# An eighth of layer 2's softmax tokens turned and summed by TensorE, and layer 3 added to the output by GpSimd's DMA

## The chip, the core and the metric

The program runs on one core of a Trainium2 chip. A core has five engines with instruction queues of their own: PE (TensorE, matrix products), DVE (VectorE), ACT (ScalarE), POOL (GpSimd) and SP (SyncE, which here only issues transfers). Each takes its instructions in order. Transfers between DRAM and the on-chip memory SBUF run on 16 DMA engines; PE writes its products to PSUM, where DVE and ACT read them. The metric is the device time of one execution in microseconds (us), as the median of several runs.

## The reference

x holds 16 images of 64x64 tokens with 256 channels, fp32. Four layers follow each other, each of the form x = x + layer(groupnorm(x)):

```
x = x + L0(gn(x))   # nearest of 1024 code vectors, by token
x = x + L1(gn(x))   # attention along each row of the image, sigmoid in place of softmax
x = x + L2(gn(x))
x = x + L3(gn(x))   # linear attention, 4 heads of 32, projected and layer-normed

def L2(x):                                # n = 4096 tokens of an image
    x0, x1, x2 = x @ w1 + b1, x @ w2 + b2, x @ w3 + b3    # one number per token each
    sim = x0[:, :, None] * x1[:, None, :]                 # n x n
    sm = softmax(sim, axis=1)                             # over the first n
    feats = einsum('bn,bnm->bm', x2, sm)
    return sigmoid(feats)[..., None] * x

def L3(x):
    q, k, v = split(x @ w_qkv)
    q = softmax(q, over the head's 32) * 32 ** -0.5
    k = softmax(k, over the tokens)
    o = (k.T @ v, by head) applied to q, then @ w_out + b_out
    return layernorm(o) * gamma + beta
```

So layer 2 takes 4096 x 4096 exponentials per image, their sum over the first index (the denominator) and their sum weighted by x2 (the numerator).

## The kernel before

An image (in the code a batch, `b`) is 8 chunks of 512 tokens. Except in the first layer's output, activations lie with channels on the 128 partitions, as two halves of 128 channels by 512 tokens (`[P, NK, CW]`, 512 KB a chunk). Each stage reads its input from a DRAM buffer and writes its output to one.

- `stats0` (L313) reads x and takes the statistics of the first group norm.
- `stage1` (L329) is the search: 32 steps per batch. A step has four fp32 matmuls into a 1024-column PSUM tile `pd` (L403), a sum and maximum on DVE (L409), the index of the maximum (L414), and a gather by POOL that adds the code vectors to the tokens (L415). `back` (L374) turns a finished chunk.
- `layer1` (L441) does the row attention. Its `ph` and `po` tiles are the other users of 1024-column PSUM tiles, of which there are two (`ps_w`, L68); the four 512-column ones come from `ps_m` (`bank`).
- `rows2` (L567) makes x0, x1 and x2 for the batch and writes them to DRAM; `spread_rows` (L610) reads x0 and x2 back, repeated on all partitions, 2048 tokens at a time (two halves).
- `stage2` (L620) is the softmax. A tile has 128 values of the second index on the partitions and 2048 of the first along the row. ACT takes the exponentials with x1 as the factor and the row's sum as a by-product (L645); DVE multiplies by x2 and sums (L648). There are 32 x 2 such tiles per batch, in three buffers `ex`. Then the gate is made and stored.
- `gate2` (L681) applies the gate, takes statistics, and stores the residual x3 to DRAM (L709).
- `stage3` (L717) is layer 3. A first pass over the chunks loads x3 (L760) and makes keys, queries, values and the context; `put_row` puts the constant row `x_row` together (L788). A second pass, the out pass, makes the output: for each pair of 128 tokens PE turns x3 back to tokens on the partitions (L902), adds the projection (L908) and the constant row (L912); ACT copies the sum out of PSUM to `y` (L913) and SP stores it (L923, L926). The scale by token comes from `form`, `variance` and `deviate` (L855 to L870), with a power on POOL (L868).

The stages of up to several batches run beside each other. Every stage is a generator that yields costs; at the end of the kernel a heap interleaves them by planned start and length (L925 to L968), and the framework's scheduler then orders each engine's instructions. SP's queue holds nearly all loads and stores, and a transfer that has to wait holds up those behind it. POOL's queue holds the gathers, layer 3's differences and products on the queries (L802, L756) and the powers.

The lines that the out pass and the softmax turn on:

```
nc.scalar.activation(
    ex, x0b, AF.Exp, bias=nmax[:, T : T + 1], scale=x01[:, T, 1:2], accum_out=den[:, h, T : T + 1]
)
...
nc.tensor.matmul(px, lhsT=ones3, rhs=twice(x_row), start=False, stop=True, skip_group_check=True)
nc.scalar.copy(y[:, 2 * pr : 2 * pr + 2, :], px)
```

## Time and profile before

| | |
|---|---|
| median of 3 runs (5653.28 to 5692.56) | 5671.16 us |
| the profiled execution | 5674.06 us |
| its span, first to last instruction | 5672.1 us |
| mean granted TensorE clock | 0.962 |
| moved by DMA, HBM read and written | 751.18 MB and 303.04 MB |
| waits of POOL's gathers for their indices (L415 for L414) | 1337.5 us |

Times are in us unless marked ns. PEld is PE's loading of weights, which overlaps its products. In a line of a group stand the source line, the engine, the operation, the output and inputs by name, the shapes, and the count; behind the bar the busy time of all, the mean ns of one, the idle time of the engine just before them, and what ended that idle time. A wait line names who waited for whom, the total, how often and the longest. SPq and POOLq are the queues that issue transfers. Matmuls overlap: the mean ns of one is longer than the time from one start to the next.

### The profile page before, as it was taken

To read this page: it belongs to the slowest core of one execution; us is meant where nothing else is said; L and a number is where in the kernel's file an instruction comes from. 1 tells how busy PE (TensorE), PEld (TensorE's weight loads), DVE (VectorE), ACT (ScalarE), POOL (GpSimd) and SP (SyncE) were. 2 spreads that over 40 slices of the span, in tenths; PEclk is the share of its full clock that TensorE was granted. 3 is DMA by queue.
4 is the path that set the end of the run, shared out by engine and by line. 5 is a ranking of instruction groups with operands and counts; after the bars stand their busy time and mean duration, and the time that the engine had idled before them with its cause. 6 is when DMAs were issued, how large, how long until landed. Compare 5 with 4: busy or idle time off the path is not lost.

```text
span 5672.1 us, 76096 instructions
## 1 busy us (share of the span) xinstructions
PE 5162.0 (91%) x26927; PEld 3189.6 (56%) x26927; DVE 5049.3 (89%) x7186; ACT 4571.1 (81%) x6642; POOL 1801.5 (32%) x1076
## 2 busy tenths in 40 slices
PE   7977889989999999999999999999999999987788
PEld 3534446545656566565655656565565656564556
DVE  7589799899999999999999999999999999988882
ACT  4468589888989898888978888898888879887873
POOL 2223234323333333334333333333333333321221
PEclk9988999999999999999999999999999999998889
DMA  8553744655665757566575656657575675745543
GB/s 254 174 178 84 232 115 144 214 163 185 196 198 175 224 159 236 171 211 198 185 234 155 216 185 200 210 173 236 160 224 183 201 219 156 222 149 176 200 157 119
DMA packets 521365, 1059.26 MB, mean 187 GB/s; under 512 B 52504, under 2 KB 266392, under 8 KB 512792
## 3 DMA queue, kind: packets, MB, share of 16 engines
q1 hardware_dynamic: 406288, 885.11, 46.5%
q0 software_dynamic: 73728, 67.14, 8.3%
q10 hardware_dynamic: 40968, 102.13, 4.6%
q8 instruction: 214, 3.51, 0.3%
q14 instruction: 167, 1.37, 0.1%
HBM read 751.18 MB, written 303.04 MB: 186 GB/s over the span
## 4 chain that ended last, share of the span: by engine, by line
PE 46%; DVE 17%; ACT 16%; issue 6%; DMA 5%; POOL 4%; SPq 0%; ACTq 0%; DVEq 0%; POOLq 0%
PE pd_s L403 14%; ACT ex_s L645 7%; DVE ex_s L648 7%; PE ph_l L493 4%; PE pxo_s L908 3%; PE pqv_s L782 3%; PE po_l L533 2%; PE pk_s L765 2%; ACT nn_s L398 2%; POOL qv_s L802 2%; PE pz_s L857 2%; DVE i_s L414 2%; DVE nn_s L409 2%; PE pxo_s L902 2%; PE pvr_s L865 2%
## 5 line engine op out<-in xcount | busy, mean ns | idle before, releaser
L648 DVE CUSTOM_DVE_ANT_0 ex_s<-ex_s,x2b 128x2048 f32<-128x2048 f32 x1024 | 2360.4, 2312 | 77.6 <-ACT ex_s L645 74.6
L645 ACT ACTIVATE ex_s<-x0b,nmax_s,x_r 128x2048 f32<-128x2048 f32 x1024 | 2138.6, 2089 | 40.7 <-DVE num_s L648 30.5
L403 PE MATMUL pd_s<-e,xn_s 128*128 128x512 f32 x4096 | 1971.1, 614 | 43.9 <-DVE m L409 27.9
L415 POOL DMA_INDIRECT xc_s<-in_emb_rows,i_s x512 | 1113.7, 2175 | 1852.7 <-DVE i_s L414 1337.5
L403 PEld LDWEIGHTS pd_s<-e,xn_s 128*128 128x128 f32 x4096 | 745.8, 195 | 778.8 <-issue 669.1
L409 DVE CUSTOM_DVE_ANT_0 nn_s<-pd_s,nn_s 128x1024 f32<-128x1024 f32 x512 | 619.9, 1212 | 113.5 <-PE pd_s L403 63.0
L414 DVE FIND_INDEX8 i_s<-m,nn_s 128x8 uint32<-128x1024 f32 x512 | 622.9, 1217 | 0.0
L398 ACT ACTIVATE nn_s<-ne,nx_s 128x1024 f32<-128x1024 f32 x512 | 582.5, 1143 | 33.1 <-DVE nx_s L369 18.7
L493 PE MATMUL ph_l<-wh_l,xt_l 128*128 128x256 f32 x2048 | 519.6, 390 | 28.7 <-DVE m L409 16.9
L782 PE MATMUL pqv_s<-wqv_s,xk_s 128*128 128x256 f32 x2048 | 489.3, 381 | 0.0
L493 PEld LDWEIGHTS ph_l<-wh_l,xt_l 128*128 128x128 f32 x2048 | 379.7, 192 | 138.9 <-issue 69.0
L782 PEld LDWEIGHTS pqv_s<-wqv_s,xk_s 128*128 128x128 f32 x2048 | 389.1, 191 | 120.6 <-issue 59.7
L802 POOL TENSOR_TENSOR qv_s<-qv_s,qm_s 128x512 f32<-128x512 f32 x128 | 221.6, 1731 | 662.6 <-DVE qm_s L801 363.2
L868 POOL TENSOR_TENSOR lrs_s<-lrs_s,mhalf 128x4 f32<-128x4 f32 x128 | 178.0, 1391 | 677.2 <-ACT lrs_s L867 663.3
L756 POOL TENSOR_TENSOR qv_s<-qv_s,qd_s 128x512 f32<-128x512 f32 x128 | 214.4, 1675 | 249.0 <-DVE qd_s L755 132.0
L533 PE MATMUL po_l<-blk,h_l 128*128 128x128 f32 x2048 | 282.1, 288 | 3.0 <-DVE m L409 1.5
L533 PEld LDWEIGHTS po_l<-blk,h_l 128*128 128x128 f32 x2048 | 260.6, 200 | 41.1 <-issue 24.5
L908 PE MATMUL pxo_s<-wctx_s,qo_s 128*128 128x256 f32 x1024 | 269.2, 386 | 2.2 <-DVE qo_s L876 2.2
L765 PE MATMUL pk_s<-xk_s,wk_s 128*128 128x512 f32 x512 | 256.0, 620 | 1.0 <-DMA xk_s<-x_g 0.9
L913 ACT COPY y_s<-pxo_s 128x512 f32<-128x512 f32 x256 | 147.5, 580 | 132.4 <-PE pxo_s L912 116.0
L378 PE MATMUL pt_s<-ident,xc_s 128*128 128x128 f32 x1024 | 156.7, 282 | 105.2 <-DMA xc_s<-in_emb_rows,i_s 79.0
L351 ACT ACTIVATE sq_s<-xt_s,first 128x512 f32<-128x512 f32 x256 | 200.2, 806 | 37.2 <-DMA x0b<-rows_r 21.0
(206 smaller groups left out, 7322.0 us busy)
## 6 DMA issues: line engine op xcount, KB each, us to landing
xs_s<-in_xT SPq DMA_DIRECT2D x128, 512.0 KB
xt_s<-in_xT SPq DMA_DIRECT2D x128, 512.0 KB
xc_s<-in_x SPq DMA_DIRECT2D x128, 512.0 KB
x_s<-xt_s ACTq DMA_DIRECT2D x128, 512.0 KB
xt_l<-x_s SPq DMA_DIRECT2D x128, 512.0 KB
x_l<-xt_l SPq DMA_DIRECT2D x128, 512.0 KB
xr_r<-x_l SPq DMA_DIRECT2D x128, 512.0 KB
xg_g<-x_l SPq DMA_DIRECT2D x128, 512.0 KB
```

The costliest lines, as they stand in the source:

```text
L398: nc.scalar.activation(nn, ne2, AF.Identity, bias=nx2[ch][:, t : t + 1])
L403: nc.tensor.matmul(pd[:, cols], lhsT=xn[ch][:, k, t * P : (t + 1) * P], rhs=e2[:, k, cols], start=(k == 0), stop=(k == NK - 1),)
L409: nc.vector.tensor_tensor_reduce(out=nn, in0=pd, in1=nn, scale=1.0, scalar=-3.0e38, op0=ALU.add, op1=ALU.max, accum_out=m8[:, 0:1],)
L414: nc.vector.max_index(i8, m8, nn)
L415: nc.gpsimd.indirect_dma_start(out=xc[ch][:, t, :], out_offset=None, in_=emb_rows, in_offset=bass.IndirectOffsetOnAxis(ap=i8[:, 0:1], axis=0),
L493: nc.tensor.matmul(ph[:, t, :], lhsT=X[:, k, t * P : (t + 1) * P], rhs=wh_n[:, k, :], start=(t % 2 == 0 and k == 0), stop=False, skip_grou ...
L533: nc.tensor.matmul(po[:, m : m + P], lhsT=h[:, t, k * P : (k + 1) * P], rhs=at[:, t, :, :].rearrange("p r i -> p (r i)"), start=True, stop ...
L645: nc.scalar.activation(ex, x0b, AF.Exp, bias=nmax[:, T : T + 1], scale=x01[:, T, 1:2], accum_out=den[:, h, T : T + 1])
L648: nc.vector.tensor_tensor_reduce(out=ex, in0=ex, in1=x2b, scale=1.0, scalar=0.0, op0=ALU.mult, op1=ALU.add, accum_out=num[:, h, T : T + 1],)
L765: nc.tensor.matmul(pk, lhsT=wk_n[:, k, :], rhs=xt[:, k, :], start=(k == 0), stop=(k == NK - 1))
L782: nc.tensor.matmul(pqv[:, j, :], lhsT=xt[:, k, t * P : (t + 1) * P], rhs=wqv_n[:, k, :], start=(j == 0 and k == 0), stop=False, skip_group ...
L908: nc.tensor.matmul(px[:, j, :], lhsT=qT[:, t * P : (t + 1) * P], rhs=wctx[:, 1, :], start=False, stop=False, skip_group_check=True,)
```

## The change

Layer 2: the last 4 of the 32 groups of 128 tokens of the first index (an eighth, `SHARE`) leave the tiles of the second half, which become 1536 wide. For them the matrix is formed turned: first index on the partitions, second along the row. `parts_of_rows` splits x1, the negated maximum and x0 into three bf16 parts each, sends the parts through DRAM to 12 partitions, and `outer` makes their products and sums in PSUM, 1024 columns at a time. ACT takes the plain exponential (`powers`), PE sums over the partitions with a column of x2 and one of ones (`contract`), ACT copies, PE turns the rows back and DVE sums four parts (`collect`). Each of the 8 chunks of the second index gets one such sequence, spread over the steps of the softmax.

Layer 3: `gate2` stores its residual straight to the output, which now lies in chunks with channels on the partitions. The out pass no longer loads x3, turns it or adds the constant row. It makes the projection with channels on the partitions, ACT adds the constant as a bias by partition, and a transfer that POOL issues adds the chunk to what lies in the output. The output is put in the reference's order after the launch, where it is reshaped.

```
+SHARE = 4
+SHARES = {}
+PROD = 12
...
+    spread = const.tile([P, 2, P], BF16, name="spread")
+    nc.gpsimd.memset(spread, 0.0)
+    for g in range(4):
+        nc.gpsimd.memset(spread[32 * g : 32 * g + PARTS], 1.0)
+    pair = const.tile([P, 8, 32], F32, name="pair")
+    nc.gpsimd.memset(pair, 0.0)
+    nc.gpsimd.memset(pair[:, :, 1], 1.0)
...
     def spread_rows(rd, b, h):
+        width = TOK // 2 - (P * SHARES.get(b, SHARE) if h == 1 else 0)
...
     def stage2(b, parts=1):
...
+        sums = small.tile([P, 2, 3, NT], F32, tag="sums", name=f"sums_{tag}", bufs=1)
...
+        def parts_of_rows():
+            nc.vector.tensor_copy(cat[:, 0:NT], x01[:, :, 1])
+            nc.vector.tensor_copy(cat[:, 2 * NT : 2 * NT + K], x01[:, NT - K :, 0])
+            nc.vector.tensor_copy(pair[:, 0:K, 0], x01[:, NT - K :, 2])
+            n = 2 * NT + K
+            pp = bank(f"pcat_{tag}")
+            nc.tensor.transpose(pp[:n, :P], cat[:, :n], ident)
+            bits = small.tile([2 * NT + 8, PARTS, P], BF16, tag="bits", name=f"bits_{tag}", bufs=1)
+            for m in range(PARTS):
+                nc.vector.tensor_copy(bits[:n, m, :], pp[:n, :P])
+                if m + 1 < PARTS:
+                    nc.vector.tensor_tensor(pp[:n, :P], pp[:n, :P], bits[:n, m, :], ALU.subtract)
+            ud = dram.tile([1 + PARTS, PARTS, NT, P], BF16, tag="ud", name=f"ud_{tag}")
+            nc.sync.dma_start(out=ud[0].rearrange("m t p -> t m p"), in_=bits[NT : 2 * NT])
+            for m in range(PARTS):
+                nc.sync.dma_start(out=ud[1 + m].rearrange("m t p -> t m p"), in_=bits[0:NT])
+            vd = dram.tile([PARTS, PARTS, 8, P], BF16, tag="vd", name=f"vd_{tag}")
+            for m in range(PARTS):
+                nc.sync.dma_start(out=vd[:, m, 0:K].rearrange("m t p -> t m p"), in_=bits[2 * NT : n])
+            for g in range(4):
+                nc.sync.dma_start(
+                    out=spread[32 * g + PARTS : 32 * g + PROD, 0 : K // 4, :],
+                    in_=vd.rearrange("i m (e g) p -> (i m) g e p", g=4)[:, g, 0 : K // 4, :],
+                )
+            return ud
+
+        def begin(c):
+            u = s2p.tile([P, CW], BF16, tag="uu", name=f"uu_{tag}_{c}", bufs=2)
+            src = ud.rearrange("i m t p -> (i m) (t p)")[:, c * CW : (c + 1) * CW]
+            for g in range(4):
+                nc.sync.dma_start(out=u[32 * g : 32 * g + PROD, :], in_=src)
+            others[c] = u
+
+        def outer(c, n):
+            e, q = divmod(n, 2)
...
+            pw = wide(f"pet_{tag}_{c}_{n}")
+            for r in range(2):
+                g = 2 * q + r
+                rows = slice(32 * g, 32 * g + PROD)
+                nc.tensor.matmul(
+                    pw[:, r * CW : (r + 1) * CW], lhsT=spread[rows, e, :], rhs=u[rows, :], start=True, stop=True
+                )
+            banks[c, n] = pw
+
+        def powers(c, n):
+            e, q = divmod(n, 2)
+            if q == 0:
+                others[c].append(s2p.tile([P, TOK // 2], F32, tag="ex", name=f"et_{tag}_{c}_{e}", bufs=3))
+            nc.scalar.activation(others[c][-1][:, 2 * q * CW : 2 * (q + 1) * CW], banks.pop((c, n)), AF.Exp)
+
+        def contract(c):
+            pn = bank(f"pn_{tag}_{c}")
+            for e in range(K // 4):
+                for g in range(4):
+                    nc.tensor.matmul(
+                        pn[32 * g : 32 * g + 32, :], lhsT=pair[:, 4 * e + g, :],
+                        rhs=others[c][1 + e][:, g * CW : (g + 1) * CW], start=(e == 0), stop=(e == K // 4 - 1),
+                    )
+            nc.scalar.copy(others[c][-1][:, 0:CW], pn)
+
+        def collect(c):
+            row = others.pop(c)[-1]
+            pt = bank(f"pnt_{tag}_{c}")
+            for t in range(CH):
+                nc.tensor.transpose(pt[:, t * P : (t + 1) * P], row[:, t * P : (t + 1) * P], ident)
+            nc.vector.tensor_reduce(
+                sums[:, :, 2, c * CH : (c + 1) * CH].rearrange("p r t -> p t r"),
+                pt.rearrange("p (t j n) -> p t n j", j=4, n=32)[:, :, 0:2, :], AX.X, ALU.add,
+            )
...
-                    yield 2.4
+                    yield 2.4 * width / (TOK // 2)
+                    c = part + step // 8
+                    n = step % 8
+                    if K == 0:
+                        pass
+                    elif n <= K // 2:
+                        if n > 0:
+                            powers(c, n - 1)
+                            yield 1.2
+                        if n < K // 2:
+                            outer(c, n)
+                    elif n == 5:
+                        contract(c)
+                        if c + 1 < NCHUNK:
+                            begin(c + 1)
+                    elif n == 7:
+                        collect(c)
+                    step += 1
...
     def gate2(b):
...
-            d = dram.tile([P, NK, CW], F32, tag=f"x3_{ch}", name=f"x3_{tag}_{ch}", bufs=3)
-            nc.sync.dma_start(out=d, in_=xt)
-            x3.append(d)
+            nc.sync.dma_start(out=dst[ch], in_=xt)
...
     def stage3(b):
...
-            if ch == 0:
-                put_row(x_row, xm_, by_identity, f"x_{tag}", idle=8)
...
-            xt = xb.tile([P, NK, CW], F32, tag="xb", name=f"xo_{tag}_{ch}")
-            nc.sync.dma_start(out=xt, in_=x3[ch])
             qT = qs[ch]
-            y = s3p.tile([P, CH, C], F32, tag="u4", name=f"y_{tag}_{ch}")
-            for pr in range(2):
+            y = s3p.tile([P, NK, CW], F32, tag="u4", name=f"y_{tag}_{ch}")
+            for pr in range(NK):
                 if pr == 1 and ch + 1 < NCHUNK:
                     deviate(ch + 1)
-                px = bank(f"pxo_{tag}_{ch}_{pr}").rearrange("p (j c) -> p j c", c=C)
-                for j in range(2):
-                    t = 2 * pr + j
-                    for k in range(NK):
-                        nc.tensor.matmul(
-                            px[:, j, k * P : (k + 1) * P], lhsT=xt[:, k, t * P : (t + 1) * P], rhs=ident,
-                            is_transpose=True, start=(j == 0 and k == 0), stop=False, skip_group_check=True,
-                        )
-                for j in range(2):
-                    t = 2 * pr + j
-                    nc.tensor.matmul(
-                        px[:, j, :], lhsT=qT[:, t * P : (t + 1) * P], rhs=wctx[:, 1, :], start=False, stop=False,
-                        skip_group_check=True,
-                    )
-                nc.tensor.matmul(px, lhsT=ones3, rhs=twice(x_row), start=False, stop=True, skip_group_check=True)
-                nc.scalar.copy(y[:, 2 * pr : 2 * pr + 2, :], px)
+                px = bank(f"pxo_{tag}_{ch}_{pr}")
+                nc.tensor.matmul(px, lhsT=wctx[:, 1, pr * P : (pr + 1) * P], rhs=qT, start=True, stop=True)
+                nc.scalar.activation(y[:, pr, :], px, AF.Identity, bias=xm_[:, pr : pr + 1])
...
-                    if before is not None:
-                        nc.sync.dma_start(out=dst[:, (ch - 1) * CH : ch * CH, :], in_=before)
+                    nc.gpsimd.dma_start(out=x3[ch], in_=y, accum_op=ALU.add)
```

## The prediction

> **What bounds the kernel now.** I read the page's busy times first, then the busy times by stretch, the waits of PE and DVE in the steady stretch, the groups by line in that stretch, and last the timeline of PE in the middle and at the end.
>
> ```profile
> PE 5162.0 (91%) x26927; PEld 3189.6 (56%) x26927; DVE 5049.3 (89%) x7186; ACT 4571.1 (81%) x6642; POOL 1801.5 (32%) x1076
> ```
>
> Over the whole span PE and DVE are close together. The stretch from 1500 to 4900 us says more (columns: length, then busy us of PE, weight loads, DVE, ACT, POOL, then PE clock, DMA share, GB/s):
>
> ```profile
> 1500.00:4900.00 3400.00, 3222.50 (x17247) 2013.05 (x17246) 3187.87 (x4508) 2910.59 (x4229) 1169.16 (x669) 0.99 0.63 197
> ```
>
> The groups in the same stretch:
>
> ```profile
> L648 DVE CUSTOM_DVE_ANT_0 ex_s<-ex_s,x2b 128x2048 f32<-128x2048 f32 x656 | 1513.5, 2311 | 55.9 <-ACT ex_s L645 53.3 <-issue 2.5
> ...
> L908 PE MATMUL pxo_s<-wctx_s,qo_s 128*128 128x256 f32 x692 | 178.0, 380 | 0.0
> L765 PE MATMUL pk_s<-xk_s,wk_s 128*128 128x512 f32 x320 | 153.0, 596 | 1.0 <-DMA xk_s<-x_g 0.9
> L902 PE MATMUL pxo_s<-ident,xo_s 128*128 128x128 f32 x688 | 106.9, 275 | 0.0
> ...
> L912 PE MATMUL pxo_s<-x_row,ones 128*128 128x512 bf16 x173 | 65.6, 379 | 0.0
> ...
> L593 PE MATMUL pr_r<-xr_r,wrow_n 128*32 128x512 f32 x320 | 46.2, 601 | 0.0
> ...
> L645 ACT ACTIVATE ex_s<-x0b,nmax_s,x_r 128x2048 f32<-128x2048 f32 x656 | 1370.1, 2089 | 11.1 <-DVE nmax_s L632 6.5 <-DVE num_s L648 3.2
> ```
>
> A batch has 64 of the L648 products, so 656 of them are 10.25 batches, 331.7 us each. Per batch PE is busy 314.4 us (94.8%), DVE 311.0 (93.8%), ACT 284.0 (85.6%), POOL 114.1. Neither of the first two alone is the bound: each idles some 6%. What ends their waits:
>
> ```profile
> DVE ex_s L648 <- ACT ex_s L645: 53.3, 42, 2.8
> DVE nn_s L409 <- ACT nn_s L398: 25.2, 40, 2.2
> ```
> ```profile
> PE px_s L357 <- ACT sq_s L351: 22.6, 25, 2.2
> PE pxt_s L364 <- ACT xrow_s L362: 16.1, 27, 1.6
> ```
>
> DVE waits for ACT, and next for PE (L765, 22.8 us); PE waits for ACT, and its longest wait for DVE, L493 for the search's reader, is 13.7 us. The reader is to see that relief for DVE alone can be eaten by PE.
>
> **The change, per batch.** An fp32 matmul of the source is two passes in the trace (2048 in L403 as built, 4096 rows), a transpose and a bf16 matmul are one.
>
> *Softmax, shorter half.* 32 of 64 tiles shrink from 2048 to 1536 columns. ACT: from 2089 ns at 2048 columns and 1144 at 1024 (L398), 512 columns are 0.473 us: -15.1. DVE: from 2311 and 1212 (L409), 512 columns are 0.550 us: -17.6.
>
> *Softmax, the turned eighth.* ACT: 16 exponentials of 128x1024 from PSUM, at L502's 1.013 us: +16.2; 8 copies of 128x512 at L913's 0.579: +4.6. DVE: 8 tiny reductions of a transposed bank, between the small copy L603 (0.168) and the full L801 (0.676); they read 32 values per row, so the former: +1.4. `parts_of_rows` adds three small copies (0.5) and five operations on 68x128 of PSUM, between L369 (0.15) and L809 (0.34), say 0.25: +1.2. PE: `outer` makes 16 pairs of bf16 matmuls on separate row groups; a pair costs between one L912 (0.379, fully together) and two: 6.1 to 12.1, I take the middle, 9.0. `contract` makes 32 fp32 matmuls, 64 passes, into four column groups. L593 has that form, 46.2/320 = 0.144 us each: 9.2; if they did not overlap, 153.0/320 = 0.478 each: 30.6. `collect` makes 32 transposes at L378's 0.144: 4.6, and `parts_of_rows` one more with its load: 0.3.
>
> The tiling switches show in PE's timeline (start, length, then the group):
>
> ```profile
> 4256.77 2.82 PE L403 MATMUL pd_s<-e,xn_s 128*128 128x512 f32 x6
> 4259.52 1.94 PE L593 MATMUL pr_r<-xr_r,wrow_n 128*32 128x512 f32 x16
> ```
>
> Six passes ahead of the column-tiled group take 2.75 us from start to start; elsewhere eight take 3.44 (0.43 each), so 0.17 us goes at this border. [...]
>
> *Layer 3's out pass.* Gone per batch, from the rows: (178.0 + 106.9 + 65.6)/10.25 = 34.2, and with the x row's eight idle matmuls (18.9), its weight products (6.0) and residues (5.3) 37.1. New: 16 fp32 matmuls of 512 columns, 32 passes at 0.478: +15.3. ACT: 16 copies at 0.579 become activations with a bias, between 0.600 (L746) and 0.687 (L597): +0.3, up to 1.7; the x row's casts go, 0.194 + 2 x 0.345 + 0.362: -1.2.
>
> *Sums.* DVE -17.6 + 1.4 + 0.5 + 1.2 = -14.5: 296.5 us (-10.4 with the dear reductions). PE -37.1 + 15.3 + 9.0 + 9.2 + 4.6 + 0.3 = +1.3: 315.7 (from -1.6 to +25.8 by the bounds). ACT -15.1 + 16.2 + 4.6 + 0.3 - 1.2 = +4.8: 288.8. So DVE is relieved, PE stands still, ACT gains a little.
>
> *Queues.* SP loses 256 issues (the x3 loads and the stores) and gains 43 per batch: eleven for the split rows and 32 for `begin`, each about the 0.39 us of L923. The first `begin` waits for its rows to land in DRAM, like these, and SP's later loads stand behind it:
>
> ```profile
> 1923.58 4.82 DMA rows_r<-rows_r
> ```
>
> One or two such round trips are 5 to 10 us a batch. Behind them are the search's x loads, issued two chunks ahead of a 41 us chunk (331.7/8), and layer 3's loads, in four buffers that the x3 loads no longer share. I cost it at 10 us in all; uncovered it is 160. POOL gains eight issues a batch, between SP's 0.39 and the gather's 1.62 us (median in the stretch): 13 at most, 127 of 325. Each waits for the second half of y. Behind it stand the powers of `variance` (PE's `deviate` waits for them) and the gathers (`back` waits, most of a chunk later). POOL waits anyway: 1337.5 us for indices, 663.3 for L867. Zero, up to 2 us for each, 256 in all. The transfers' engines are 63% busy; the x3 load that goes is worth the read-back that comes.
>
> *The end.* The out pass of the last batch is PE's alone:
>
> ```profile
> 5658.05 0.60 PE L902 MATMUL pxo_s<-ident,xo_s 128*128 128x128 f32 x4
> 5658.49 1.03 PE L908 MATMUL pxo_s<-wctx_s,qo_s 128*128 128x256 f32 x4
> 5659.36 0.38 PE L912 MATMUL pxo_s<-x_row,ones 128*128 128x512 bf16 x1
> 5659.57 0.95 PE L865 MATMUL pvr_s<-one,qz_s 128*128 128x1 f32 x8
> ```
>
> From L902 to L865 is 1.52 us, and it becomes 0.86: 1.32 per chunk, 10.6 over eight. The x row gives 2. The two passes before it run beside the last softmax; half of theirs, 10. The last store lands 4.2 us after its copy now; as an accumulating one it is priced by the gather's 5.4 on the chain (a quarter of the bytes) and POOL's issue, +5 together. Net -17. [...]
>
> *From engines to time.* If the batch keeps DVE's share, it takes 296.5/0.938 = 316.3 us, -15.4. If it keeps PE's, 315.7/0.948 = 333.0, +1.3. The waits name both and ACT, so I take the middle, -7.1. It counts for 10.25 batches and the 1.75 or so ahead of 1500 us: 12 x 7.1 = 85. The profiled execution took 5674.06 us (span 5672.1), 3 above the median of 5671.16. Sum: 5674 - 85 - 17 + 10 = 5582.
>
> **Rivals.** *DVE decides alone:* 12 x 15.4 = 185 off, 5482. For it: DVE's waits are short. Against: PE has no room to match without losing its idle time.
> *PE decides:* 12 x 1.3 on, 5674 + 16 - 17 + 10 = 5683, no change that shows. For it: 94.8% busy and no less work.
> *The wide PSUM buffers make it slower:* `outer` takes one of the two 1024-column buffers, 256 times, beside 768 tiles of the search and layer 1 now. In PE's order as built, with the trace's pitches, I estimate the work between a wide tile's last matmul and the first of the tile two later, which needs its buffer: under 3 us for 35 of 766 before and 236 of 1022 after; under 1.5 us for none and 91. A read alone takes 1.0 to 1.2 us and stands behind products of 2.3. At 1.5 us for the 91 and 0.5 for the other 145 it costs 209: 5791. It decides from 0.6 us per new tile (5728). Against it: DVE, which reads the search's tiles, has 14.5 us less to do per batch.
>
> **How the numbers follow.** The middle 0.50 (its own range 5530 to 5640), DVE alone 0.15, PE decides 0.20, wide buffers 0.15. A measurement of this kernel tells about 1% from no change: below 5614 is faster, above 5728 slower. Faster: 0.39 of the middle and 0.15, 0.54. Same: 0.11 + 0.16 + 0.02 = 0.29. Slower: 0.04 + 0.13 = 0.17. The range 5460 to 5730 leaves out some 0.04 below and 0.14 above.
>
> **What would show it.** DVE's product at two sizes, 2311 and about 1760 ns; DVE's busy time down by some 230 us, ACT's up by 77, PE's within 60. The column-tiled contract at 0.15 us each, not 0.48. The last out pass at 3.9 us a chunk instead of 5.2. I am wrong if PE's waits for the readers of wide tiles grow past 150 us, if the shorter products are followed by idle DVE time for ACT, or if POOL's stores hold up the gathers.

## The result, and the profile after

The changed kernel takes 5882.76 us (median of 4 runs, 5867.16 to 5891.78), the kernel before 5673.14 beside it: 1.0363 of before, 95% interval 1.033 to 1.0397. It is slower by some 210 us. The profiled execution took 5891.78 us, its span is 5890.1 us. First the page's busy times, then the stretch from 1500 to 4900 us (columns as in the prediction):

```profile
PE 5309.6 (90%) x26975; PEld 3059.2 (52%) x26975; DVE 4899.5 (83%) x7442; ACT 4670.4 (79%) x6962; POOL 1872.4 (32%) x1210
```
```profile
1500.00:4900.00 3400.00, 3183.82 (x16562) 1844.95 (x16561) 2990.54 (x4503) 2850.01 (x4263) 1199.18 (x726) 0.97 0.60 178
```

630 products on DVE in the stretch are 9.84 batches of 345.4 us; before, a batch took 331.7. Per batch PE is busy 323.4 us (+9.0), DVE 303.8 (-7.2), ACT 289.5 (+5.5). PE's share fell from 94.8% to 93.6% although its work grew, and its granted clock from 0.99 to 0.97: something new makes it stand. PE's longest wait in the stretch:

```profile
PE pgt_s L772 <- DVE gate_s L769: 80.0, 10, 11.9
```

It stands ten times, once per batch: PE waits 8.0 us on average to turn the finished gate of layer 2. In the same stretch of before PE never stood idle ahead of this transpose (the last number of its group):

```profile
L666 PE MATMUL pgt_s<-ident,gate_s 128*32 128x128 f32 x10 | 2.7, 273 | 0.0
```

PE's timeline at one of the ten:

```profile
3762.47 4.46 PE L407 MATMUL pd_s<-e,xn_s 128*128 128x512 f32 x10
3778.11 0.37 PE L772 MATMUL pgt_s<-ident,gate_s 128*32 128x128 f32 x1 [11.18 <-DVE gate_s L769]
3778.28 3.71 PE L868 MATMUL pk_s<-xk_s,wk_s 128*128 128x512 f32 x4
3781.78 3.07 PE L885 MATMUL pqv_s<-wqv_s,xk_s 128*128 128x256 f32 x8
3784.68 0.38 PE L889 MATMUL pqv_s<-qv_row,ones 128*128 128x512 bf16 x1
3784.90 1.89 PE L885 MATMUL pqv_s<-wqv_s,xk_s 128*128 128x256 f32 x8
```

The stop costs more than its length: the first keys after it take 3.71 us and the first queries 3.07, where the second group of queries takes 1.89. Over the ten stops the keys take 3.71 (once 3.67) instead of 1.88, the queries 2.43 on average instead of 1.89: 2.4 us on top of 8.0. PE's granted clock is 1.00 in the 3 us ahead of each of the ten stops and 0.50 in the 3 us after each; at the stop above it is 1.00 again from 3785 us on.

Who is late? POOL, ACT and DVE at the same place:

```profile
3755.58 1.58 POOL L635 PARTITION_ALL_REDUCE ab_s<-ext_s  x1 [9.45 <-DVE i_s L418]
...
3770.55 1.04 POOL L903 TENSOR_TENSOR qv_s<-qv_s,qm_s 128x512 f32<-128x512 f32 x1 [10.28 <-issue]
```
```profile
3771.63 0.63 ACT L904 ACTIVATE qv_s<-qv_s 128x512 f32<-128x512 f32 x1 [7.36 <-POOL qv_s L903]
...
3773.91 0.21 ACT L767 ACTIVATE gate_s<-gate_s 128x32 f32<-128x32 f32 x1
```
```profile
3767.06 0.17 DVE L766 TENSOR_TENSOR gate_s<-gate_s,nsum_s 128x32 f32<-128x32 f32 x1
3772.29 0.69 DVE L857 TENSOR_REDUCE qd_s<-qv_s 128x16 f32<-128x512 f32 x1 [5.05 <-ACT qv_s L904]
...
3774.15 0.18 DVE L768 TENSOR_SCALAR gate_s<-gate_s 128x32 f32<-128x32 f32 x1 [0.83 <-ACT gate_s L767]
3774.24 2.32 DVE L649 COPY pair<-x_r 128x4 f32<-128x4 f32 x1
3776.48 1.21 DVE L413 CUSTOM_DVE_ANT_0 nn_s<-pd_s,nn_s 128x1024 f32<-128x1024 f32 x1
...
3777.62 0.34 DVE L769 RECIPROCAL gate_s<-gate_s 128x32 f32<-128x32 f32 x1
```

The gate's argument is ready at 3767.2. Its exponential on ACT (L767) then stands behind layer 3's exponential of the queries (L904) and two more activations. L904 waits for POOL, and POOL stands idle for 10.28 us after its all-reduce for the next batch and one gather. DVE's last step (L769) stands behind `pair`, a new copy of 128x4 that takes 2.32 us here, and a search step. In these rows all four engines keep the order of their queues, and PE's transpose is the last link. Where the stretch begins, POOL's queue has two `MODIFY_POOL_CONFIG` at the line of that next product (L903), 0.63 us each, the first at 3759.77: the rows behind what the expectations call GpSimd's change of program. L903 has such a pair in twelve of the sixteen batches, and from its start to the start of the product pass 7.6 to 11.5 us. POOL stood there before too (7.5 to 10.8 us in twelve batches), but there the gate was ready when PE came to it.

Where the 218 us between the spans arise, by the moments at which ACT copies a gate (L774 and its like):

| from, to | before | changed | gate later | both later |
|---|---|---|---|---|
| start, 1st gate | 597 | 600 | 611 | 610 |
| 1st, 2nd | 420 | 450 | 451 | 441 |
| 2nd, 14th | 3945 | 4103 | 3996 | 3979 |
| 14th, 15th | 296 | 301 | 295 | 303 |
| 15th, end | 415 | 436 | 425 | 409 |

(The last two columns are the experiments `gate_later` and `both_later`. The last batch makes its gate in eight parts, which are not in the table.) 158 of the 218 us are lost in the twelve middle batches, 30 in the second, 21 at the end.

### The profile page after: what moved, and what is told of

The parts are those of the page before. It is cut to its first block, busy times and chain, and to the rows that moved or that the text cites. A ratio compares the mean times of both kernels' runs of the same rounds, so it can differ in the third digit from the quotient of the medians.

```text
span 5890.1 us, 77461 instructions
## 1 busy us (share of the span) xinstructions
PE 5309.6 (90%) x26975; PEld 3059.2 (52%) x26975; DVE 4899.5 (83%) x7442; ACT 4670.4 (79%) x6962; POOL 1872.4 (32%) x1210
## 3 DMA queue, kind: packets, MB, share of 16 engines
HBM read 682.12 MB, written 304.76 MB: 168 GB/s over the span
## 4 chain that ended last, share of the span: by engine, by line
PE 56%; DVE 18%; ACT 10%; issue 6%; DMA 5%; POOL 3%; SPq 0%; ACTq 0%; POOLq 0%; DVEq 0%
PE pd_s L407 19%; DVE ex_s L737 6%; PE ph_l L497 5%; PE pqv_s L885 4%; ACT ex_s L733 3%; PE pxo_s L997 3%; PE po_l L537 3%; PE pk_s L868 3%; DVE i_s L418 3%; DMA xc_s<-in_emb_rows,i_s 2%; DVE nn_s L413 2%; PE pz_s L958 2%; PE pn_s L703 2%; PE pc_s L908 2%; DVE xg_g L809 2%
## 5 line engine op out<-in xcount | busy, mean ns | idle before, releaser
L737 DVE CUSTOM_DVE_ANT_0 ex_s<-ex_s,x2b 128x2048 f32<-128x2048 f32 (+1 forms) x1024 | 2094.2, 2054 | 122.4 <-ACT ex_s L733 120.9
L733 ACT ACTIVATE ex_s<-x0b,cat_s,x_r 128x2048 f32<-128x2048 f32 (+1 forms) x1024 | 1921.0, 1877 | 40.8 <-DVE sums_s L737 35.5
L419 POOL DMA_INDIRECT xc_s<-in_emb_rows,i_s x512 | 1151.5, 2249 | 2006.8 <-DVE i_s L418 1309.0
L903 POOL TENSOR_TENSOR qv_s<-qv_s,qm_s 128x512 f32<-128x512 f32 x128 | 191.9, 1499 | 592.9 <-DVE qm_s L902 366.8
L1007 POOL DMA_DIRECT2D out<-y_s x128 | 128.1, 1001 | 624.0 <-ACT lrs_s L968 381.4
L697 ACT ACTIVATE et_s<-pet_s 128x1024 f32<-128x1024 f32 x256 | 259.9, 1016 | 42.0 <-PE pet_s L688 41.3
L997 PE MATMUL pxo_s<-qo_s,wctx_s 128*128 128x512 f32 x512 | 279.6, 630 | 2.2 <-ACT lrs_s L968 1.2
L859 POOL TENSOR_TENSOR qv_s<-qv_s,qd_s 128x512 f32<-128x512 f32 x128 | 172.8, 1350 | 336.1 <-DVE qd_s L858 218.3
L868 PE MATMUL pk_s<-xk_s,wk_s 128*128 128x512 f32 x512 | 274.2, 661 | 1.1 <-DMA xk_s<-out 1.1
L998 ACT ACTIVATE y_s<-pxo_s,xm_g 128x512 f32<-128x512 f32 x256 | 175.1, 684 | 118.7 <-PE pxo_s L997 103.8
```

The costliest lines, as they stand in the source:

```text
L419: nc.gpsimd.indirect_dma_start(out=xc[ch][:, t, :], out_offset=None, in_=emb_rows, in_offset=bass.IndirectOffsetOnAxis(ap=i8[:, 0:1], axis=0),
L733: nc.scalar.activation(ex, x0b, AF.Exp, bias=nmax[:, T : T + 1], scale=x01[:, T, 1:2], accum_out=sums[:, 1, h, T : T + 1],)
L737: nc.vector.tensor_tensor_reduce(out=ex, in0=ex, in1=x2b, scale=1.0, scalar=0.0, op0=ALU.mult, op1=ALU.add, accum_out=sums[:, 0, h, T : T ...
L868: nc.tensor.matmul(pk, lhsT=wk_n[:, k, :], rhs=xt[:, k, :], start=(k == 0), stop=(k == NK - 1))
L997: nc.tensor.matmul(px, lhsT=wctx[:, 1, pr * P : (pr + 1) * P], rhs=qT, start=True, stop=True)
```

## The experiments

All ratios are to the kernel before, run beside them, with 95% intervals; the changed kernel's is 1.0363.

**Layer 3's half alone.**

```
-SHARE = 4
+SHARE = 0
```

> The changed kernel with no softmax token handed to TensorE, so layer 3's half of the change by itself. Theory A (the loss is a stop of TensorE of some 8 us at the gate of each batch, which the late sum of the handed-over tokens causes): no stop at the gate beyond the 13 us of before in all, and 5,590 to 5,670 us. Theory C (the accumulating store in GpSimd's queue costs it, by late gathers and late powers): 5,740 to 5,860 us, with the waits for gathered rows and for GpSimd's power as long as in the changed kernel (107 and 41 us). Theory D (TensorE simply has to do what is put on it, 22 us less in each batch here): about 5,430 us.

5699.47 us, 1.0051 (1.0032 to 1.0071): none of the three. The stretch:

```profile
1500.00:4900.00 3400.00, 3129.66 (x15842) 1868.89 (x15841) 3164.80 (x4487) 2900.47 (x4167) 1261.11 (x749) 0.97 0.62 183
```

10.19 batches of 333.7 us: PE has 307.2 instead of 314.4, a relief of 7.2 and not of 22 (8 of the 22 were never there, as the point on PE below works out, and the clock is 0.97 instead of 0.99); DVE has 310.7 as before. There is no stop at the gate, as A says (4.8 us in the whole span), but this relief of PE brings no time. DVE is at 93% of the batch; and as this half also holds the adding stores, it is not a pure relief of PE.

**Layer 2's half alone.** The new softmax, and the old layer 3 whole; against the changed kernel:

```
-                    nc.gpsimd.dma_start(out=x3[ch], in_=y, accum_op=ALU.add)
+                    if before is not None:
+                        nc.sync.dma_start(out=dst[:, (ch - 1) * CH : ch * CH, :], in_=before)
```

and so for the rest of layer 3's part of the diff.

> The kernel before with layer 2's share alone: the old end of layer 3 with its transposes, its row of offsets and its stores from the sync queue. Theory A: the stop at the gate is there, 6 to 12 us in each batch, and the time is 5,850 to 6,000 us. Theory C: no worse than before, 5,620 to 5,720 us. Theory D: TensorE has 23 us more in each batch, 5,930 to 5,970 us, with or without a stop at the gate.

5983.68 us, 1.0543 (1.0523 to 1.0563), in A's range and 14 us above D's; PE waits 73.7 us for the gate over the span, and in the stretch 5.0 us on average at nine gates, less than the 6 to 12 that A gave. PE has 332.9 us a batch, 18.5 more than before, and a batch takes 351.5, 19.8 more. PE's added work is thus nearly as long as the loss, and the time alone does not tell A from D. C falls: without the adding stores it is slower, not faster. The stop belongs to layer 2's half.

**The gate's transpose later.**

```
-            yield 1
+            yield 1 if parts > 1 else 8
             pg = bank(f"pgt_{tag}_{part}")
```

> The changed kernel with the gate's transpose, its copy and its store some 7 places of 160, about 15 us, later in the order of the work; nothing else is moved. Theory A: TensorE's wait for the gate falls from 111 us to under 30, the matmuls after it run at full clock, and the time falls by 100 to 150 us, to 5,730 to 5,780. Theories C and D: the wait at the gate was time that TensorE would have lost elsewhere; 5,850 to 5,890 us.

5777.87 us, 1.0189 (1.0165 to 1.0212): A. Only the place of one transpose, with its copy and its store, is changed, and half the loss is gone. The same place in PE's timeline, without a wait, and with the keys in 1.88 us:

```profile
3711.79 0.27 PE L772 MATMUL pgt_s<-ident,gate_s 128*32 128x128 f32 x1
3711.90 1.88 PE L868 MATMUL pk_s<-xk_s,wk_s 128*128 128x512 f32 x4
```

A batch takes 335.3 us (649 products), 10.1 less, against 8.0 of wait and 2.4 of slow matmuls per stop. PE is now at 321.2 of 335.3, 95.8%.

**No all-reduce on GpSimd.**

```
...
+        nc.tensor.transpose(pe_[:2, :P], ext, ident)
...
+        nc.vector.tensor_reduce(top, pe_[:2, :P], AX.X, ALU.max)
...
+        nc.tensor.transpose(pa_[:, 0:2], top.to_broadcast([2, P]), ident[:2, :2])
...
-        nc.gpsimd.partition_all_reduce(ab, ext, P, bass_isa.ReduceOp.max)
+        nc.vector.tensor_copy(ab, pa_[:, 0:2])
```

> The changed kernel with the largest and smallest of layer 2's first row found without GpSimd: TensorE turns the 128 pairs, VectorE takes the maximum, TensorE turns it back to all partitions. GpSimd's change of program after the all-reduce, an idle stretch of about 10 us in each batch, should be gone. Theory A in its narrow form (the stop at the gate is made by that stretch: ScalarE's wait for GpSimd stands before the gate's exponential): the wait for the gate falls below 40 us and the time by 60 to 130 us. If the late sum alone makes the stop: the wait for the gate stays at 80 to 111 us, and the time at 5,850 to 5,890. Theory C: the gathers are no longer held behind the stretch, TensorE's wait for gathered rows falls from 107 to under 60 us, and the time by 30 to 60 us.

5850.7 us, 1.0316 (1.0297 to 1.0334). The wait for the gate falls from 111.0 to 38.5 us over the span, so POOL's stretch, with what follows from it, is most of that wait (the copy `pair` takes no more than 0.17 us there); the time falls by some 30 us only, half of what A's narrow form gives at least. That is inside C's 30 to 60, but C's sign is missing: PE's wait for gathered rows falls from 107 to 95 us and not below 60. The same edit to the kernel before:

> The kernel before with the all-reduce of GpSimd replaced as in the changed one, where that took 32 us. If GpSimd's idle stretch delays the first rows of each batch's softmax in any case: 5,640 to 5,660 us, and this beats both kernels. If before covers it: 5,670 to 5,690, and the 32 us were the share of the stop at the gate that this stretch makes.

5728.03 us, 1.0093 (1.006 to 1.0126): slower, by neither account. With two more transposes of PE at the batch's border DVE meets a wait of 39.6 us in the stretch that was not among its longest before:

```profile
DVE xg_g L709 <- ACT u_g L708: 39.6, 10, 5.0
```

Ten times, up to 5.0 us: again one stop per batch. That it makes the loss is not shown. And both edits to the changed kernel, this one and the later gate:

> The changed kernel with both mends: the gate's transpose later, and no all-reduce by GpSimd. If they mend the same stop at the gate: 5,760 to 5,780 us, no better than the later transpose alone (5,778). If GpSimd's change of program costs by itself, through late gathers at the start of each batch's softmax: 5,725 to 5,750 us.

5792.13 us, 1.0185 (1.0159 to 1.0211): no better than the later gate alone, as the first account says: they mend the same stop. As the edit by itself cost the kernel before 52 us, a gain of the same size could be hidden in this sum; no run separates the two.

**The eighth left out, nothing in its place.** In the kernel before, and in the changed one with `SHARE = 0`, one line of `spread_rows`:

```
+        width = TOK // 2 - (4 * P if h == 1 else 0)
```

> The kernel before with the last 512 tokens left out of layer 2's softmax and nothing in their place: the second product and exponential of each pair are 1536 wide, so VectorE has about 17 us and ScalarE about 15 us less in each batch, TensorE as much as before. If VectorE decides the time of before (theory V): 5,450 to 5,520 us. If TensorE alone decides it (theory P): 5,650 to 5,690. If both stand at the limit, so that relief of one alone is worth little (theory B): 5,600 to 5,680.

> The changed kernel with the last 512 tokens left out of layer 2's softmax and nothing in their place, so that both are relieved: TensorE by the new layer 3, VectorE and ScalarE by the shorter half. Theory B (both engines at the limit): the two reliefs together give what neither gives alone, some 13 us in each batch and the end, 5,450 to 5,530 us. Theory P: the relief of TensorE would have shown in layer 3's half alone, which it did not (5,699 us). If some chain of waits decides and no engine: 5,650 to 5,700 us.

5694.05 us, 1.0022 (1.001 to 1.0034), and 5626.52 us, 0.99 (0.9872 to 0.9927). The stretch of each:

```profile
1500.00:4900.00 3400.00, 3231.61 (x17082) 1993.63 (x17081) 3042.16 (x4480) 2748.79 (x4199) 1071.72 (x664) 0.99 0.62 194
```
```profile
1500.00:4900.00 3400.00, 3187.75 (x16043) 1880.47 (x16039) 3059.07 (x4576) 2808.46 (x4237) 1161.21 (x767) 0.98 0.64 184
```

The first is the case of the prediction's main term by itself: DVE has 298.2 us a batch instead of 311.0, ACT 269.4 instead of 284.0, and a batch takes 333.2 us, not less than before. Theory V falls; the time lies just above P's range and B's. With PE relieved too (304.5; DVE 292.2), a batch takes 324.8, 6.9 less: the two reliefs together give what neither gave alone, as B says, but half of B's 13, and 5626.52 us is outside every range. There is a rival to this reading, a stop. The first of the two versions has a new one, 5.4 us long in seven batches of ten:

```profile
PE pd_s L414 <- DVE m L420: 64.4, 35, 5.4
```

PE waits there for the search's reader on DVE; in the stretch of before this wait was 1.4 us. PE's busy time grows with it, from 314.4 to 316.7 us a batch. No run moved this stop, so it stays open how much of DVE's relief it ate.

**Every other batch.** The two edits (no all-reduce, later gate), and

```
-SHARES = {}
+SHARES = {b: 0 for b in (0, 1, 3, 5, 7, 9, 11, 13, 15)}
```

> The kernel with both mends, TensorE taking its eighth in seven batches of sixteen only (not in the first, nor in the odd ones). Theory B: both engines come out below before, TensorE by some 9 us a batch and VectorE by some 5, and the time is 5,590 to 5,650 us. If what the hand-over costs is in its fixed steps at the start of each batch's softmax: about half of the excess of the full share is left, 5,690 to 5,730 us.

5718.73 us, 1.0071 (1.0047 to 1.0094): in the range of the second account, and no version that beats before. Of the excess of the full share with both edits (108 us) a third is left, 35 us, for seven batches of sixteen.

**The wide buffers.**

```
-            pw = wide(f"pet_{tag}_{c}_{n}")
+            pw = []
...
+                pw.append(bank(f"pet_{tag}_{c}_{n}_{r}"))
```

> The changed kernel with each table of exponents (two products of 512 columns) in two of the four 512-column PSUM buffers instead of one of the two wide ones, and the exponential in two pieces of 512. If the two wide buffers, shared with the search's scores and layer 1, hold TensorE up (the rival of the prediction): 5,770 to 5,840 us. If they do not: 5,880 to 5,960, since ScalarE has 16 exponentials more in each batch and the four small buffers turn faster.

5862.67 us, 1.0312 (1.0286 to 1.0338), between the two; the intervals of the two kernels overlap. PE's wait for the gate stays (50.4 us in the stretch). The wide buffers are not the main cause; up to some 20 us of the loss may be theirs. The trace of the changed kernel agrees: PE's waits for the readers of wide tiles come to some 84 us over the span, 57 before, where the prediction's sign of this rival was 150.

**The sum eight steps earlier.**

```
-                    c = part + step // 8
-                    n = step % 8
-                    if K == 0:
+                    c, n = divmod(step, 7) if parts == 1 else (part, step)
+                    if K == 0 or c >= NCHUNK:
...
-                    elif n == 7:
+                    elif n == (6 if parts == 1 else 7):
```

> The changed kernel with the eight hand-overs of a batch packed into 56 of the 64 steps (seven steps each instead of eight), so that the last sum of the handed-over tokens is collected eight steps before the gate. The gate's place is not touched. If the late sum makes the stop at the gate: TensorE's wait for the gate falls from 111 to below 40 us and the time by 70 to 110 us, to 5,770 to 5,810. If the stop has another cause (GpSimd's stretch, ScalarE's order): the wait stays above 80 us and the time at 5,850 to 5,890.

5991.45 us, 1.0543 (1.0516 to 1.057): slower by 109 us, which no theory had. In the stretch:

```profile
PE pgt_s L771 <- DVE gate_s L768: 59.6, 9, 7.5
```
```profile
DVE ex_s L737 <- ACT ex_s L733: 116.4, 100, 2.8
```

The wait for the gate falls by a quarter only, so the late sum is not what makes the stop; that part of A falls. Other waits grow (DVE's for ACT from 43.4 to 116.4). With the later gate, and no hand-over in the first two batches:

> The changed kernel with the earlier sum, the later transpose of the gate, and no hand-over in the first two batches, where it costs 30 us by the distance between the first two gates. What is left is TensorE's work, 4 to 7 us more in each batch of the steady stretch than before: 5,710 to 5,745 us. If below 5,670, the hand-over itself would be worth its place.

5928.66 us, 1.0441 (1.0416 to 1.0466), some 185 us above what was expected. PE's longest wait in the stretch is now at the other transpose of the border, that of the packed rows (`pcat`):

```profile
PE pcat_s L652 <- DVE cat_s L648: 71.4, 10, 9.5
```

Is it the place of a hand-over inside the beat of the search that costs? In the kernel with the later gate, moved by two steps:

```
-                    elif n <= K // 2:
+                    elif 2 <= n <= K // 2 + 2:
...
```

> The changed kernel with the gate's transpose later, and each hand-over moved by two of its eight steps against the rest of the work (outer products at steps 2 and 3, exponentials at 3 and 4, the sum at 6, its collection at 7 as before). If the place inside the beat of the search matters, as the loss by seven steps instead of eight suggests (5,991 against 5,883 us): a difference of over 25 us from 5,778. If not: 5,765 to 5,790, and the loss by seven steps has another cause.

5791.01 us, 1.0191 (1.0161 to 1.0221), against 5778: the place does not matter by itself. Why seven steps lose stays open.

**The store by SP, not adding** (layer 3's part alone reaches the output):

```
-                    nc.gpsimd.dma_start(out=x3[ch], in_=y, accum_op=ALU.add)
+                    if before is not None:
+                        nc.sync.dma_start(out=x3[ch - 1], in_=before)
...
```

> The changed kernel with layer 3's result stored by the sync queue, one chunk later as in the kernel before, and not added to what lies in the output (the output lacks the residual): GpSimd issues 128 stores less, and the second read of 67 MB is gone. Theory C (the adding store costs by GpSimd's queue and by traffic): 5,780 to 5,850 us, with less waiting for GpSimd's power and for gathered rows. If it is hidden: 5,870 to 5,890.

5859.23 us, 1.0313 (1.029 to 1.0335), between the two accounts: some 25 us, with intervals that touch. The stop at the gate is there (72.2 us in the stretch). The second read of 67 MB that the expectation names is its author's estimate and was not shown: the changed kernel's page counts 682.12 MB read from HBM, 69.1 less than before, where the x3 loads that went are 67.1.

**The share in the middle batches only**, with the later gate:

```
-SHARES = {}
+SHARES = {0: 0, 1: 0, 15: 0}
```

> The changed kernel with the gate's transpose later, and no hand-over in the first two batches and the last one. By the distances between the gates, the later transpose alone (5,778 us) is behind layer 3's half alone (5,699) by 46 us up to the second gate, by some 21 over the steady batches and by 21 after the last: if the hand-over costs only where nothing else runs beside it, 5,695 to 5,725 us. If its cost moves on to the first batch that has it: 5,750 to 5,780.

5739.44 us, 1.0095 (1.0064 to 1.0126): 39 us less than with the hand-over everywhere (5778), between the two accounts: between the first two gates lie 438 us, where the later gate alone has 451 and layer 3's half alone 418, so the hand-over explains less than half of that excess.

**No sums.** Later gate; contraction and collection left out, so that the gate lacks the eighth:

```
                     elif n == 5:
-                        contract(c)
+                        others.pop(c)
...
-                    elif n == 7:
-                        collect(c)
```

> The changed kernel with the gate's transpose later, and the handed-over tokens' exponentials made but never summed (the contraction and the collecting transposes are left out, so the gate lacks these tokens): TensorE has some 15 us less in each batch, ScalarE 5 and VectorE 1. If TensorE decides the changed kernel: 5,640 to 5,680 us. If the chain of steps decides and not TensorE's work: 5,740 to 5,780.

5740.76 us, 1.0107 (1.0079 to 1.0136). PE has 310.7 us a batch instead of 321.2, and a batch takes 336.3, where it took 335.3 with the sums; the 37 us that the whole gains on `gate_later` lie outside the stretch. The reason is seen in PE's waits:

```profile
PE pcat_s L652 <- DVE cat_s L648: 77.1, 10, 8.2
```

The same stop at the border, now at `pcat`. If that is what ate the relief, placing `pcat` later must free it:

```
             nc.vector.tensor_copy(pair[:, 0:K, 0], x01[:, NT - K :, 2])
+            yield 6
             n = 2 * NT + K
...
-        yield 2
+        if not K:
+            yield 2
...
```

with the hand-overs two steps on, so that their rows arrive in time, and the later gate; once with the sums and once without:

> The changed kernel with the gate's transpose later, the hand-overs moved by two steps, and the transpose of the packed rows and columns at the start of each batch's softmax four places of 160 later too. In the run without this last move TensorE waited 30 us at that transpose in the steady batches (5,791 us). If such a stop costs more than its wait, as the gate's did (80 us of waiting, 105 us of time): 5,745 to 5,765 us. If it stands where TensorE would wait in any case: 5,775 to 5,800.

> The same with the handed-over tokens never summed (contraction and collecting transposes left out, the gate lacks these tokens). In the run without sums before, the 15 us that TensorE had less in a batch came out as 3 us, and TensorE waited 77 us at the transpose at the start of the softmax, 10 times. If that stop ate the relief: with the stop away 5,610 to 5,670 us. If TensorE's work does not decide: 5,710 to 5,750.

5740.43 us, 1.0108 (1.0086 to 1.013), and 5643.67 us, 0.9945 (0.9924 to 0.9966): the first 5 us below its first account, the second within it. The two stretches:

```profile
1500.00:4900.00 3400.00, 3293.82 (x17120) 1912.62 (x17118) 3043.75 (x4643) 2949.15 (x4396) 1182.22 (x749) 0.97 0.63 182
```
```profile
1500.00:4900.00 3400.00, 3243.19 (x16456) 1905.66 (x16453) 3091.82 (x4649) 2953.15 (x4408) 1302.27 (x768) 0.97 0.65 186
```

With both transposes placed after their inputs, a batch takes 334.8 us at 324.3 of PE (96.9%), and 325.7 at 310.7: now 13.6 us less of PE's busy time give 9.1 of time, where 10.5 gave nothing while the stop at `pcat` stood. ACT has 7.5 us less as well and DVE 3.5. So, once these stops are gone, TensorE's work decides the changed kernel for the most part; that ACT's share in the 9.1 is small is argued, not shown. Of the versions that compute everything the kernel before stays the fastest: their ratios all lie over 1.

## Why the prediction was wrong

It gave 5582 us and a range to 5730; the time is 5883. The step that failed is "From engines to time": "The waits name both and ACT, so I take the middle, -7.1". The batch became 13.7 us longer. Beside it PE's sum, "+1.3", was mis-sized, and a wait that the sum put at nothing came.

- *Half of the middle was DVE's share, and that relief brought nothing by itself.* `cut_alone` takes the softmax's eighth away from DVE and ACT and gains no time (1.0022), perhaps in part because of its own new stop. In before PE and DVE both stand at 94%, and load on PE costs time although DVE is relieved: with the gate later PE has 6.8 more a batch, DVE 9.6 less, and the batch is 3.6 longer. At their shares of before, PE's 321.2 would make 338.8 us and DVE's 301.4 would make 321.3. The batch took 335.3, near the later of the two and not at their mean. The rival "PE decides" (5683) stood for that.
- *That rival missed the stop, and so did its opposite.* The rival on the slow side looked for PE's new waits at the wide buffers; `banks` moves the time by 20 us. The wait that came is at a transpose of 0.37 us that the change does not touch, whose input came later by a new order behind POOL and, in this version, a new copy (`sum_earlier` and `layer2_alone` stop 5.0 to 6.6 us with that copy at 0.16 us, so the copy is not what makes the stop). It costs 10.1 us a batch in the steady stretch (`gate_later`), and 105 us in all. The prediction never asked, for the single small instructions at a batch's border, which result they wait for and who stands behind them on PE.
- *PE +1.3* was +9.0, and +6.8 with the gate later; the 2.2 between them are about the 2.4 of the slow matmuls after the stops. What was mis-sized is the out pass. "Gone per batch, from the rows" adds the busy times of L902, L908 and L912, and these overlap: in the prediction's own rows they are 0.60, 1.03 and 0.38 us, 2.01 in all, but only 1.52 pass from L902's start to L865's. The new pair takes 0.86 (the last rows of this part). From start to start the out pass gives back 16 x 0.66 = 10.6 us a batch, as the prediction itself counts it for the end, and not 34.2 - 15.3 = 18.9. With these 8.3 us the sum is +9.6, and "PE decides" gives 5674 + 12 x 9.6 - 17 + 10 = 5782. That `gate_later` took 5778 is in part luck, since its steady batch is only 3.6 us longer. The new work came near by its rows: 10.7 for `contract` (said 9.2; 0.166 us a pass), 6.9 for `outer` (9.0), 4.8 for `collect` (4.6), 17.0 for the projection (15.3). Over the span PE is up by 148 us, where at most 60 were to show the sum right.
- *The borders of `outer`* are not seen in the length of its own rows but in the starts around them:

```profile
3799.54 1.12 PE L407 MATMUL pd_s<-e,xn_s 128*128 128x512 f32 x2
3800.60 0.39 PE L688 MATMUL pet_s<-uu_s,spread 12*128 12x512 bf16 x1
3800.92 2.84 PE L407 MATMUL pd_s<-e,xn_s 128*128 128x512 f32 x6
3803.69 0.39 PE L688 MATMUL pet_s<-uu_s,spread 12*128 12x512 bf16 x2
```

  From start to start two passes take 1.06 us instead of 0.86, six take 2.77 instead of 2.58, and L688 holds PE for 0.32 us, where L889, also bf16 with 512 columns, held it for 0.22 above. A visit of `outer` so costs some 0.3 us at its two borders, an estimated 4.8 us for 16 visits a batch; four more borders in each of the 8 chunks, at the 0.17 us of the prediction's row, would be an estimated 5.4. With 16 x 0.22 for the products `outer` takes an estimated 8.3, below the middle of 9.0, which so covers the borders.
- *DVE -14.5* was -7.2: the wide products took 2378 ns instead of 2311 (2.1 us a batch), `pair` 2.32 us (0.17 said), and L809 909 ns (811 before). These three make 5.9 of the 7.3 us.

```profile
L737 DVE CUSTOM_DVE_ANT_0 ex_s<-ex_s,x2b 128x2048 f32<-128x2048 f32 x310 | 735.8, 2378 | 9.3 <-ACT ex_s L733 9.3
L737 DVE CUSTOM_DVE_ANT_0 ex_s<-ex_s,x2b 128x1536 f32<-128x1536 f32 x320 | 555.1, 1748 | 34.6 <-ACT ex_s L733 34.0
L809 DVE SCALAR_TENSOR_TENSOR xg_g<-xg_g,gn_nm_n,u_g 128x512 f32<-128x512 f32 x156 | 137.4, 909 | 0.0
...
L649 DVE COPY pair<-x_r 128x4 f32<-128x4 f32 x10 | 23.2, 2324 | 0.0
```

- *ACT +4.8* was +5.5; the copy with a bias took 684 ns, the upper bound.
- *POOL's stores at zero*: some 25 us (`sync_store`), inside the 256 that was said, and hardly told from nothing. By PE's wait for gathered rows, 104 us there and 107 in the changed kernel, they did not hold up the gathers. *SP's 10 us* were not tried alone. The second batch, 30 us longer by its gates, was not seen at all.
- *The end, -17*: from the 15th gate on layer 3's half alone is 11 us shorter (404 us), the changed kernel 21 longer. The out pass takes 4.57 us a chunk, not 3.9:

```profile
5867.45 1.02 PE L997 MATMUL pxo_s<-qo_s,wctx_s 128*128 128x512 f32 x2
5868.31 0.95 PE L966 MATMUL pvr_s<-one,qz_s 128*128 128x1 f32 x8
...
5871.53 0.65 PE L976 MATMUL pdv_s<-ident,lrs_s 128*128 128x128 f32 x4 [0.45 <-POOL lrs_s L969]
5872.02 1.02 PE L997 MATMUL pxo_s<-qo_s,wctx_s 128*128 128x512 f32 x2
```

From one L997 at the head to the next: the pair takes the 0.86 that was forecast, but PE waits 0.45 us and more for POOL's power in each chunk.

Shown: the stop at the gate is half of the loss (`gate_later`), and what is left goes for the most part with PE's work (`both_later_no_sums`). Shown for the versions run, but not apart from the stops and stores that came with them: that relief of one engine alone brings nothing. Shown in the trace, and in part by `after_no_allreduce`: the chain that makes the gate late. Open: why seven steps lose 109 us, why two transposes for the all-reduce cost the kernel before 52 us, what DVE's relief gives without the new stop of `cut_alone`, and what the 30 us in the second batch are made of.

## What to carry to other kernels

Where two engines are each busy for 94% of a stage, do not take the mean of the two forecasts: expect little from the relief of one and time from load on either, until an experiment that leaves the work out says otherwise. Price matmuls from start to start, since their busy times overlap (here 2.01 us of them in 1.52). Then look at the single small instructions that the busiest engine has at a stage's border: for each, follow its input back through every queue, because one that comes 8 us late stops all that stands behind it. Before a redesign is judged by its time, move such an instruction a few places: here that alone was worth half of the loss, and a second one (`pcat`) let a relief through that had come to nothing in the steady batch.

## What the runs showed of the hardware

- After 6.3 to 11.9 us without work TensorE ran the next four passes of keys in 3.71 us (once 3.67) instead of 1.88, at a granted clock of 0.50 instead of 1.00. The ten stops were 8.0 us long on average and cost 2.4 more by slow matmuls; without them a batch was 10.1 us shorter.
- POOL stood for 10.28 us after an all-reduce and one gather before its next product. In the twelve batches of the changed kernel that have a `MODIFY_POOL_CONFIG` at L903, the product started 7.6 to 11.5 us after it; in the kernel before (L802, twelve batches) 8.0 to 11.3.
- A DVE copy of 128x4 (`pair`) took 2.32 to 2.34 us in eleven of the changed kernel's sixteen batches, ten of them in the stretch, and 0.16 to 0.17 in the other five; L648, of the same size, took 0.10. In each of the eleven a product of POOL (L859) ran beside it, and the copy ended 0.04 us after that product did; in the five none did. In `sum_earlier` and `layer2_alone` the copy never took more than 0.28 us.
- Between two visits of L688, whose operands lie on 12 partitions, two passes of the search took 1.06 us from start to start instead of 0.86 and six 2.77 instead of 2.58, and L688 held PE for 0.32 us where L889, as long a matmul on 128 partitions, held it for 0.22.
- The last adding store of 512 KB ended the span 7.6 us after its issue began (5882.48).
